# A graph network of four layers: six transfers a block moved to GpSimd's queue, a refinement in five VectorE operations, and diffusion halves added by GpSimd

## The chip, the core and the metric

The kernel runs on one core of one Trainium2 chip. A core has five engines with a queue each: TensorE (PE in the profile; its weight loads are PEld), VectorE (DVE), ScalarE (ACT), GpSimd (POOL) and SyncE (SP). Each queue is worked through in order, and semaphores make an instruction wait for another queue. Transfers between SBUF and HBM are issued from a queue (SP, ACT or POOL) and carried out by 16 DMA engines that all queues share. The metric is the device time of one execution in microseconds (us); lower is better.

## The reference

Input are 4096 nodes with 256 features and a 4096 x 4096 adjacency of zeros and ones. Four layers follow each other, each as `x = layernorm(x + layer(x, adj))`: an attention over neighbours with 8 heads (layer 0), a product with the adjacency (layer 1), the layer that matters here (layer 2), and a product with the adjacency divided by the degrees (layer 3). Layer 2 makes two steps:

```python
R = S + eye(N); R = R / R.sum(-1, keepdims=True)      # S is the adjacency
Xf = X; Xa = X; Z = 0
for n in range(2):
    A = top_p_attention(Xa, W1, W2, W3)
    Xf = R @ Xf
    Xa = A @ Xa
    Z = Z + Xf @ U1[n].T + Xa @ U2[n].T
h = layernorm(X + Z) * ln_g + ln_b
```

`top_p_attention` takes the softmax of all 4096 logits of a row, keeps the largest probabilities until their sum reaches 0.9, sets the others to zero and divides by the sum of what is kept. `R @ Xf` is called the diffusion below.

## The kernel before

The nodes are cut into 32 blocks of 128 rows. Layer 2 runs its two steps one after the other; in each, a loop over b goes through the blocks (`for b in range(NB - 1)`, under `tc.manual_schedule`, which keeps the instructions of PE, ACT, DVE and POOL in the order in which the program writes them). An iteration is a software pipeline with eight slots s = 0 to 7. In it

- the scores of block b+2 are made: four products (L933) of four matmuls on TensorE, two in slot 0 and two in slot 1, into PSUM tiles `ps_logit` of which there are two, and after each an exponential on ScalarE (L937) that writes 1024 columns of the row's weights `e` and sums them. The third product needs the tile that the first exponential has read, the fourth the second's;
- the threshold of block b+2 is guessed on ScalarE (`guessed`): a first cut c1 from the sum, two passes over `e` in two halves each (L1030, outputs `ja`), which give the count and the sum S1 above c1, and a chain of operations on one column (most through the helper `fma`, L946), which gives a better cut `c`. In step 2 a tail follows (L1052 to L1059), which makes the slopes `gw` and `sq` for one more refinement;
- the cut of block b+1 is settled on VectorE (`nucleus`). In step 2 it first takes the sum S2 of all weights above `c` in one pass of 4096 columns (L953), then refines the cut in seven operations on one column (L1077 to L1083) to `hi`. Then both steps gather the largest weights below `hi` (L1092, L1096, L1104, L1106), find by how many the sum 0.9 is reached (`bef` is the sum before them, L1112 and L1113, and so on to L1143), and zero what falls away (L1147);
- block b's weights are transposed on TensorE (L1286), copied by ScalarE (L1288, `aT`) and multiplied with X (L1295) into `ps_a`, of which there is one;
- the diffusion of block b+2 is made (L179) from pieces of the adjacency that SP's queue loads, into `ps_r`;
- the diffusion of block b+1 is finished (`diffused`): XD holds its operand split into a high and a low part, so that `ps_r` has two halves of 256 columns. ScalarE scales the low half (L1329), VectorE scales the high half and adds the low (L1331), and GpSimd adds the sum to `xb`, which `base` has loaded (L1317, L1332). In step 2 `keep` stores it (L1338);
- in step 2, block b-1 is closed (`closing`): ScalarE scales `ps_a` into `h` (L1434), GpSimd adds the loaded `xb` (`bases`, L1323; the add is L1438) and normalises twice with VectorE's statistics (L85, L86) and its own operations (L88, L89, L96, L1441, L1442); the result is stored (L1446). Block b-2 then makes its part of layer 3's operands (`turned`, `weighted`, `ahead3`; stores in L1457 and L1458).

So step 2 has six transfers a block beside those on SP's queue, and they are all issued from ScalarE's queue: L1338 in slot 4, L1457, L1458, L1317 and L1323 in slot 6, L1446 in slot 7. The tail of the guess runs where the loop finishes the generator at the head of slot 0, ahead of the scores:

```python
pa = ps1.tile([P, 512], F32, name="ps_a")
whole(guessing)
guessing = guessed(step, b + 2) if ahead else iter(())
if s < 2 and ahead:
    next(score)
    next(score)
```

Outside the block loops a scheduler orders the instructions.

Of the kernel before, what the change touches and what calls it, by code (L numbers as in the profile page):

```python
# [9 lines left out]
F32 = mybir.dt.float32  # L10
# [7 lines left out]
ALU = mybir.AluOpType  # L18
# [5 lines left out]
P = 128  # L24
# [31 lines left out]
class Net:  # L56
# [686 lines left out]
    def layer2(self):  # L743
# [3 lines left out]
        with ExitStack() as ctx:  # L747
# [40 lines left out]

            consts = [math.log(math.sqrt(2 * math.pi) / N), *QUANTILE, -FEW, 0.5 * N, 14.0, 0.75, 0.5, 400.0, CENTRAL[1]]
            cs = pool.tile([P, len(consts)], F32, name="cs")  # L790
# [178 lines left out]
            def guessed(step, b):  # L969
# [75 lines left out]

                c, gw, sq, lows = (small(n, bufs=2) for n in ("c3", "gw", "sq", "lows"))
                ic = small("ic")
                fma(c, low, -1.0, c2, AF.Relu)
                fma(c, c, 1.0, low)
                nc.scalar.mul(lows, c, 0.3)  # L1050
                yield c, lows, far, thr, S1, gw, sq
                nc.scalar.activation(ic, c, AF.Ln)  # L1052
# [8 lines left out]
            def nucleus(step, b, c, low, far, thr, S1=None, gw=None, sq=None):  # L1061

# [9 lines left out]
                if step == 0:  # L1072
                    nc.vector.tensor_scalar(hi, c, low, far, op0=ALU.max, op1=ALU.mult)
                else:
                    d = small("d")
                    S2 = evaluate("S2", e, c)
                    nc.vector.scalar_tensor_tensor(d, S1, S2, gw, op0=ALU.subtract, op1=ALU.mult)  # L1077
# [235 lines left out]
            def base(step, b):  # L1313


                xb = work.tile([P, 2, D], F32, name="xb", bufs=2)
                nc.scalar.dma_start(xb[:, 0], xd[b, :, 0, :] if step else pd[b])  # L1317
                return xb

            def bases(b):  # L1320

                xb = work.tile([P, 2, D], F32, name="xb", bufs=2)
                nc.scalar.dma_start(xb, xd[at(b)].rearrange("o p s d -> (o p) s d"))  # L1323
                return xb

            def diffused(b, pr, xb):

                dif = work.tile([P, D], F32, name="dif", bufs=1)
                nc.scalar.mul(dif, pr[:, D:], rdeg[:, at(b)])  # L1329
                yield  # L1330
                nc.vector.scalar_tensor_tensor(dif, pr[:, :D], rdeg[:, at(b)], dif, op0=ALU.mult, op1=ALU.add)  # L1331
                nc.gpsimd.tensor_add(xb[:, 0], xb[:, 0], dif)  # L1332

            def keep(step, b, xb):

                if step == 1:
                    yield
                    nc.scalar.dma_start(xd[b, :, 0, :], xb[:, 0])  # L1338
                    return
                part = work.tile([P, 2, D], F32, name="part", bufs=1).bitcast(F32R)  # L1340
                nc.scalar.copy(part[:, 0], xb[:, 0])
                yield
                nc.vector.tensor_sub(part[:, 1], xb[:, 0], part[:, 0].bitcast(F32))
                yield
                nc.scalar.dma_start(xfd[b], part.bitcast(F32))
# [83 lines left out]

            def closing(b, pa, r, xb, hand=None):  # L1430

# [17 lines left out]
            def ahead3(b, h, pz, last=False):  # L1449

                part = XD[:, b] if last else work.tile([P, 2, D], F32, name="part", bufs=1).bitcast(F32R)
                nc.scalar.copy(part[:, 0], pz[:, D:])
                nc.scalar.copy(h[:, 0], pz[:, :D])
                nc.vector.tensor_sub(part[:, 1], pz[:, D:], part[:, 0].bitcast(F32))
                yield
                if not last:
                    nc.scalar.dma_start(xtd[at(b)].rearrange("o p s d -> (o p) s d"), part.bitcast(F32))  # L1457
                nc.scalar.dma_start(xo[at(b), :, 1].rearrange("o p d -> (o p) d"), h[:, 0])  # L1458

# [11 lines left out]
            for step in range(2):  # L1471
# [25 lines left out]
                pr = whole(diffusion(step, 0))  # L1497
                whole(diffused(0, pr, xb))
                whole(keep(step, 0, xb))
# [5 lines left out]
                with tc.manual_schedule(engines={ET.PE, ET.Activation, ET.DVE, ET.Pool}):  # L1505
                    for b in range(NB - 1):
# [6 lines left out]
                        for s in range(8):  # L1513
                            if s == 0:
                                if b:
                                    if step == 0:
                                        store(b - 1, pa, rs.pop(b - 1))
                                    else:
                                        close = closing(b - 1, pa, rs.pop(b - 1), xc)
                                        next(close)  # L1520
                                difs = diffused(b + 1, pr, xb)
# [20 lines left out]
                            if s == 3 and step == 1 and b - 2 in done:  # L1542
                                put = ahead3(b - 2, done.pop(b - 2), pz)
                                next(put)
# [10 lines left out]
                            if s == 6:  # L1555
                                if ahead:
                                    xb = base(step, b + 2)
                                if step == 1:
                                    xc = bases(b)
                            if s >= 2 and ahead:  # L1560
# [169 lines left out]
```

## Time and profile before

| | us |
|---|---|
| median of 3 runs (4158.45 to 4166.36) | 4163.09 |
| the profiled execution | 4162.25 |
| its span, first to last instruction | 4160.5 |
| busy: PE, DVE, ACT, POOL | 3926.9, 3051.4, 2748.5, 958.6 |
| step 1's block loop, by the profile | about 1832 to 2720 |
| step 2's block loop, by the profile | about 2847 to 3861 |

A page of the profile gives busy time for each engine, groups of instructions by source line (L1295 is line 1295 of the kernel before), what ended an engine's idle time, and a timeline. "e<-e,edge" names an instruction by the tiles it writes and reads; ACTq or POOLq is the queue's own work, such as issuing a transfer. A wait for several semaphores is put down to the one that came last. Lines in step 2 that matter: L953 takes 4.49 us on VectorE each time, L1030 2.0 us on ScalarE, L937 1.02, L1438 3.97 on GpSimd with a shortest of 0.72.

### The profile page before, as it was taken

The page shows a single profiled execution, that of the slowest core. Times are in us where ns is not written, and L with a number is a line of the kernel's source. Part 1 is how long each engine was busy: PE and PEld are TensorE (multiplying, and loading weights), DVE is VectorE, ACT ScalarE, POOL GpSimd, SP SyncE. Part 2 cuts the span into 40 slices and gives each one's busy share as a digit, 9 for nine tenths or more (in the row PEclk, how much of TensorE's full clock was granted, in tenths as well). Part 3 has the DMA queues.
Part 4 walks back from the last instruction along what each step waited for, and adds up shares of the span by engine and source line. Part 5 has one row for each costly group of instructions (what it writes and reads, how often), then busy time and mean ns, then how long its engine had stood idle before and what let it go on. Part 6 is the DMA issues. An engine that isn't in the chain of part 4 may idle for free. (4 is left out here: it accounts for less than half of the span.)

```text
span 4160.5 us, 68601 instructions
## 1 busy us (share of the span) xinstructions
PE 3926.9 (94%) x25081; PEld 3380.1 (81%) x25081; DVE 3051.4 (73%) x6882; ACT 2748.5 (66%) x5103; POOL 958.6 (23%) x954
## 2 busy tenths in 40 slices
PE   7999989999997999799999999899999999998799
PEld 6999989999997787478888888656777777777587
DVE  7643239999998444658888888756999999999354
ACT  5543339999996322468888888545887878876232
POOL 0111110110333122200110110013444444444111
PEclk9999999999998999999999999999999999999899
DMA  4765554224320796333333333444333333334341
GB/s 124 226 206 179 177 200 158 80 82 164 91 71 18 282 377 232 91 120 101 94 96 102 95 94 104 147 130 122 103 96 102 102 108 102 97 102 150 133 136 46
DMA packets 303608, 545.13 MB, mean 131 GB/s; under 512 B 38294, under 2 KB 134038, under 8 KB 299158
## 3 DMA queue, kind: packets, MB, share of 16 engines
q1 hardware_dynamic: 200068, 367.08, 27.7%
q10 hardware_dynamic: 87506, 125.11, 8.8%
q0 software_dynamic: 15680, 48.38, 3.7%
q8 instruction: 203, 3.33, 0.3%
q14 instruction: 151, 1.24, 0.1%
HBM read 374.51 MB, written 165.94 MB: 130 GB/s over the span
## 5 line engine op out<-in xcount | busy, mean ns | idle before, releaser
L1295 PE MATMUL ps_a<-X,aT 128*128 128x256 f32 x4096 | 977.7, 381 | 17.4 <-ACT h L1434 15.3
L1295 PEld LDWEIGHTS ps_a<-X,aT 128*128 128x128 f32 x4096 | 772.6, 190 | 153.7 <-ACT h L1434 27.3
L300 PE MATMUL acc<-gm,gt 128*128 128x198 bf16 x8192 | 705.7, 249 | 26.1 <-issue 14.9
L300 PEld LDWEIGHTS <-gt 128*128 128x128 fp8e4 x8192 | 701.9, 97 | 29.9 <-issue 15.0
L292 ACT ACTIVATE sg<-lpb,nlc 128x1024 fp8e4<-128x1024 f32 x640 | 671.3, 1135 | 59.4 <-DVE gt L294 34.4
L179 PE MATMUL ps_r<-XD,adj_piece 128*128 128x512 f32 x2048 | 576.5, 416 | 8.1 <-DMA adj_piece<-adjs 5.0
L517 PE MATMUL pz<-src,ar 128*128 128x264 f32 x4096 | 511.4, 288 | 10.7 <-DVE ar L507 8.2
L517 PEld LDWEIGHTS pz<-src,ar 128*128 128x128 f32 x4096 | 508.4, 190 | 13.5 <-DVE ar L507 11.9
L1030 ACT ACTIVATE ja<-e,nc 128x2048 uint8<-128x2048 f32 x240 | 481.2, 2005 | 52.5 <-DMA xtd<-part 34.1
L1288 ACT COPY aT<-ps_tp 128x512 f32<-128x512 f32 x512 | 298.0, 582 | 246.6 <-PE ps_tp L1286 233.2
L179 PEld LDWEIGHTS ps_r<-XD,adj_piece 128*128 128x128 f32 x2048 | 364.5, 190 | 86.7 <-issue 14.3
L510 ACT ACTIVATE nb<-a 128x512 uint8<-128x512 f32 x256 | 156.6, 630 | 293.7 <-DMA a<-in_adjt_dram 287.1
L1096 DVE MAX8 cand<-v 128x8 f32<-128x256 f32 x1024 | 347.3, 414 | 4.4
L1147 DVE SCALAR_TENSOR_TENSOR e<-e,edge 128x512 f32<-128x512 f32 x512 | 344.9, 747 | 2.2
L203 ACT ACTIVATE adj_piece<-na 128x1024 fp32r<-128x1024 fp8e4 x128 | 135.3, 1059 | 317.9 <-PE ps_adj L731 132.7
L1286 PE MATMUL ps_tp<-ident,e 128*128 128x128 f32 x2048 | 309.8, 274 | 6.6 <-ACTq L1159 3.2
L933 PE MATMUL ps_logit<-kT,q 128*128 128x512 f32 x1024 | 276.7, 411 | 33.5 <-ACT e L937 27.3
L1092 DVE SCALAR_TENSOR_TENSOR v<-e,hi 128x2048 f32<-128x2048 f32 x128 | 305.9, 2390 | 2.3
L1286 PEld LDWEIGHTS ps_tp<-ident,e 128*128 128x128 f32 x2048 | 257.6, 142 | 60.6 <-issue 4.1
L285 DVE TENSOR_SCALAR sg<-lpb,nlc 128x1024 fp8e4<-128x1024 f32 x384 | 283.4, 775 | 2.0
L937 ACT ACTIVATE e<-ps_logit 128x1024 f32<-128x1024 f32 x256 | 259.5, 1023 | 19.0 <-PE ps_logit L933 17.1
L507 DVE CAST ar<-a 128x1024 fp32r<-128x1024 f32 x128 | 88.7, 693 | 230.7 <-PE pz L517 230.7
(341 smaller groups left out, 5445.9 us busy)
## 6 DMA issues: line engine op xcount, KB each, us to landing
adj_piece<-adjs SPq DMA_DIRECT2D x512, 256.0 KB
a<-in_adjt_dram SPq DMA_DIRECT2D x256, 256.0 KB
adjs<-adj_piece SPq DMA_DIRECT2D x96, 512.0 KB
na<-nad SPq DMA_DIRECT2D x64, 512.0 KB
na<-nad ACTq DMA_DIRECT2D x32, 1024.0 KB
nad<-nb POOLq DMA_DIRECT2D x128, 128.0 KB, 3.3
lpb<-lpd POOLq DMA_DIRECT2D x32, 512.0 KB, 4.3
gmd<-gb ACTq DMA_DIRECT2D x64, 198.0 KB
```

Of the source, the lines that this page charges most:

```text
L179: nc.tensor.matmul(ps, a[:, k, :], rhs(jc).rearrange("p s d -> p (s d)"), start=(jc == 0), stop=(jc == self.NB - 1))
L285: nc.vector.tensor_scalar(sg[:, k, :], lpb, nlc[:, jc, h:h + 1], 2.0 ** -5, op0=ALU.is_ge, op1=ALU.mult, saturate=False)
L292: nc.scalar.activation(sg[:, k, :], lpb, AF.Sign, scale=-1.0, bias=nlc[:, jc, h:h + 1], saturate=False)
L300: nc.tensor.matmul(acc[:, q, :6 * C1], gt[:, k, q * P:(q + 1) * P], gm[:, jc, hh, :], start=(jc == 0 and q % 2 == 0), stop=(jc == NB - 1 a ...
L517: nc.tensor.matmul(pz[q][:, t, :W], ar[:, q, k, :], src[:, jc, t, s], start=(jc == 0 and s == 0), stop=(jc == NB - 1 and s == 1))
L1030: nc.scalar.activation(ja, e[:, s * HALF:(s + 1) * HALF], f, bias=nc1, accum_out=fs[:, i + s:i + s + 1])
L1092: nc.vector.scalar_tensor_tensor(v, ec, hi, ec, op0=ALU.is_lt, op1=ALU.mult, accum_out=sb[:, s:s + 1])
L1096: nc.vector.max(cand[:, 8 * j:8 * j + 8], v[:, k * 256:(k + 1) * 256])
L1147: nc.vector.scalar_tensor_tensor(ec, ec, edge[:, j:j + 1], ec, op0=ALU.is_ge, op1=ALU.mult)
L1286: nc.tensor.transpose(pt[:, k * P:(k + 1) * P], e[:, jc * P:(jc + 1) * P], self.ident)
L1288: nc.scalar.copy(aT, pt)
L1295: nc.tensor.matmul(pa[:, :D], aT[:, k * P:(k + 1) * P], X[:, jc, :], start=(jc == 0), stop=(jc == NB - 1))
```

## The change

In step 2 the six transfers of a block are issued from GpSimd's queue. The refinement is written as `hi = max(c + (S2 - thr) * sq / (S2 * gw - pm), low) * far` with gw of the opposite sign and a new column pm = S1 * gw - 400 made by ScalarE: five VectorE operations instead of seven. The two operations of `bef` become one, in both steps. In step 2 ScalarE scales both halves of the diffusion in one operation of 512 columns, and GpSimd adds the halves to `xb` one after the other; VectorE no longer takes part. The tail of the guess is moved behind the first product and exponential of slot 0. `xT` has one buffer instead of two, and `dif` is twice as wide. What is left out below is one more constant (-400) and the new argument `step` or `queue` where these functions are called.

```diff
                 nc.scalar.mul(lows, c, 0.3)
-                yield c, lows, far, thr, S1, gw, sq
+                yield c, lows, far, thr, pm, gw, sq
                 nc.scalar.activation(ic, c, AF.Ln)
                 nc.scalar.activation(ic, ic, AF.Exp, scale=-1.0)
-                fma(gw, S1, 1.0, nthr)
+                fma(gw, S1, -1.0, thr)
                 nc.scalar.mul(gw, gw, ic)
                 nc.scalar.activation(sq, gw, AF.Square)
                 nc.scalar.mul(gw, gw, ic)
+                fma(pm, S1, gw, cs[:, 13:14])
                 fma(sq, sq, 1.0, cs[:, 11:12])
                 nc.scalar.mul(sq, sq, ri)
...
                     S2 = evaluate("S2", e, c)
-                    nc.vector.scalar_tensor_tensor(d, S1, S2, gw, op0=ALU.subtract, op1=ALU.mult)
-                    nc.vector.tensor_scalar_add(d, d, 400.0)
+                    nc.vector.tensor_scalar(d, S2, gw, pm, op0=ALU.mult, op1=ALU.subtract)
                     nc.vector.reciprocal(d, d)
-                    nc.vector.tensor_mul(d, sq, d)
-                    nc.vector.scalar_tensor_tensor(hi, S2, thr, d, op0=ALU.subtract, op1=ALU.mult)
-                    nc.vector.tensor_scalar(hi, hi, c, low, op0=ALU.add, op1=ALU.max)
-                    nc.vector.tensor_mul(hi, hi, far)
+                    nc.vector.tensor_scalar(hi, S2, thr, sq, op0=ALU.subtract, op1=ALU.mult)
+                    nc.vector.scalar_tensor_tensor(hi, hi, d, c, op0=ALU.mult, op1=ALU.add)
+                    nc.vector.tensor_scalar(hi, hi, low, far, op0=ALU.max, op1=ALU.mult)
...
-                nc.vector.scalar_tensor_tensor(bef[:, 0:1], sb[:, 0:1], -1.0, Z, op0=ALU.mult, op1=ALU.add)
-                nc.vector.tensor_sub(bef[:, 0:1], bef[:, 0:1], sb[:, 1:2])
+                nc.vector.tensor_scalar(bef[:, 0:1], Z, sb[:, 0:1], sb[:, 1:2], op0=ALU.subtract, op1=ALU.subtract)
...
-                nc.scalar.dma_start(xb[:, 0], xd[b, :, 0, :] if step else pd[b])
+                if step:
+                    nc.gpsimd.dma_start(xb[:, 0], xd[b, :, 0, :])
+                else:
+                    nc.scalar.dma_start(xb[:, 0], pd[b])
                 return xb
 
-            def bases(b):
+            def bases(b, queue=nc.scalar):
...
-                nc.scalar.dma_start(xb, xd[at(b)].rearrange("o p s d -> (o p) s d"))
+                queue.dma_start(xb, xd[at(b)].rearrange("o p s d -> (o p) s d"))
...
-            def diffused(b, pr, xb):
-
-                dif = work.tile([P, D], F32, name="dif", bufs=1)
-                nc.scalar.mul(dif, pr[:, D:], rdeg[:, at(b)])
+            def diffused(step, b, pr, xb):
+
+                dif = work.tile([P, 2, D], F32, name="dif", bufs=1)
+                if step == 1:
+                    nc.scalar.mul(dif.rearrange("p s d -> p (s d)"), pr, rdeg[:, at(b)])
+                    yield
+                    for s in (1, 0):
+                        nc.gpsimd.tensor_add(xb[:, 0], xb[:, 0], dif[:, s])
+                    return
+                nc.scalar.mul(dif[:, 1], pr[:, D:], rdeg[:, at(b)])
                 yield
-                nc.vector.scalar_tensor_tensor(dif, pr[:, :D], rdeg[:, at(b)], dif, op0=ALU.mult, op1=ALU.add)
-                nc.gpsimd.tensor_add(xb[:, 0], xb[:, 0], dif)
+                nc.vector.scalar_tensor_tensor(dif[:, 0], pr[:, :D], rdeg[:, at(b)], dif[:, 1], op0=ALU.mult, op1=ALU.add)
+                nc.gpsimd.tensor_add(xb[:, 0], xb[:, 0], dif[:, 0])
...
                 if step == 1:
                     yield
-                    nc.scalar.dma_start(xd[b, :, 0, :], xb[:, 0])
+                    nc.gpsimd.dma_start(xd[b, :, 0, :], xb[:, 0])
                     return
...
-                xT = work.tile([P, 2, P], F32, name="xT")
+                xT = work.tile([P, 2, P], F32, name="xT", bufs=1)
...
-                nc.scalar.dma_start(xo[at(b), :, 0].rearrange("o p d -> (o p) d"), hb)
+                queue.dma_start(xo[at(b), :, 0].rearrange("o p d -> (o p) d"), hb)
...
-                    nc.scalar.dma_start(xtd[at(b)].rearrange("o p s d -> (o p) s d"), part.bitcast(F32))
-                nc.scalar.dma_start(xo[at(b), :, 1].rearrange("o p d -> (o p) d"), h[:, 0])
+                    queue.dma_start(xtd[at(b)].rearrange("o p s d -> (o p) s d"), part.bitcast(F32))
+                queue.dma_start(xo[at(b), :, 1].rearrange("o p d -> (o p) d"), h[:, 0])
...
                                 pa = ps1.tile([P, 512], F32, name="ps_a")
-                                whole(guessing)
-                                guessing = guessed(step, b + 2) if ahead else iter(())
+                                if not ahead:
+                                    whole(guessing)
+                                    guessing = iter(())
                             if s < 2 and ahead:
                                 next(score)
+                                if s == 0:
+                                    whole(guessing)
+                                    guessing = guessed(step, b + 2)
                                 next(score)
```

More of the change, by code (lines that the diff above doesn't have):

```diff
@@ L787, in layer2 @@
             kT = pool.tile([P, N], F32R, name="kT")
-            consts = [math.log(math.sqrt(2 * math.pi) / N), *QUANTILE, -FEW, 0.5 * N, 14.0, 0.75, 0.5, 400.0, CENTRAL[1]]
+            consts = [math.log(math.sqrt(2 * math.pi) / N), *QUANTILE, -FEW, 0.5 * N, 14.0, 0.75, 0.5, 400.0, CENTRAL[1], -400.0]
             cs = pool.tile([P, len(consts)], F32, name="cs")
@@ L1043, in guessed @@
                     return
-                c, gw, sq, lows = (small(n, bufs=2) for n in ("c3", "gw", "sq", "lows"))
+                c, gw, sq, pm, lows = (small(n, bufs=2) for n in ("c3", "gw", "sq", "pm", "lows"))
                 ic = small("ic")
@@ L1057, in guessed, with nucleus @@
                 nc.scalar.mul(gw, gw, ic)
+                fma(pm, S1, gw, cs[:, 13:14])
                 fma(sq, sq, 1.0, cs[:, 11:12])
                 nc.scalar.mul(sq, sq, ri)
-            def nucleus(step, b, c, low, far, thr, S1=None, gw=None, sq=None):
+            def nucleus(step, b, c, low, far, thr, pm=None, gw=None, sq=None):
                 e = es[b % 3][:, :N]
@@ L1428, in store, with closing @@
                 nc.scalar.dma_start(xad[at(b)].rearrange("o p d -> (o p) d"), h[:, 0])
-            def closing(b, pa, r, xb, hand=None):
+            def closing(b, pa, r, xb, hand=None, queue=nc.scalar):
                 h = work.tile([P, 1, D], F32, name="h", bufs=3)
@@ L1445, in closing, with ahead3 @@
                 yield
-                nc.scalar.dma_start(xo[at(b), :, 0].rearrange("o p d -> (o p) d"), hb)
+                queue.dma_start(xo[at(b), :, 0].rearrange("o p d -> (o p) d"), hb)
                 return h
-            def ahead3(b, h, pz, last=False):
+            def ahead3(b, h, pz, last=False, queue=nc.scalar):
                 part = XD[:, b] if last else work.tile([P, 2, D], F32, name="part", bufs=1).bitcast(F32R)
@@ L1497, in layer2 @@
                 pr = whole(diffusion(step, 0))
-                whole(diffused(0, pr, xb))
+                whole(diffused(step, 0, pr, xb))
                 whole(keep(step, 0, xb))
@@ L1518, in layer2 @@
                                     else:
-                                        close = closing(b - 1, pa, rs.pop(b - 1), xc)
+                                        close = closing(b - 1, pa, rs.pop(b - 1), xc, queue=nc.gpsimd)
                                         next(close)
-                                difs = diffused(b + 1, pr, xb)
+                                difs = diffused(step, b + 1, pr, xb)
                                 next(difs)
@@ L1542, in layer2 @@
                             if s == 3 and step == 1 and b - 2 in done:
-                                put = ahead3(b - 2, done.pop(b - 2), pz)
+                                put = ahead3(b - 2, done.pop(b - 2), pz, queue=nc.gpsimd)
                                 next(put)
@@ L1558, in layer2 @@
                                 if step == 1:
-                                    xc = bases(b)
+                                    xc = bases(b, nc.gpsimd)
                             if s >= 2 and ahead:
```

## The prediction

> **What bounds the kernel now.** First I read the stretches of 104 us, to find the second step of layer 2 and to see which engine is full there. Columns: stretch, its length, then busy time of PE, PEld, DVE, ACT and POOL, each with its count, the granted clock, the DMA share and GB/s. The first row is from step 1's block loop, the second from step 2's.
>
> ```profile
> 2288.00:2392.00 104.00, 104.00 (x527) 88.60 (x526) 87.00 (x249) 88.90 (x195) 11.82 (x8) 1.00 0.31 95
> 3328.00:3432.00 104.00, 99.99 (x486) 81.33 (x486) 97.30 (x260) 82.87 (x195) 43.47 (x34) 1.00 0.36 107
> ```
>
> In step 1 TensorE never rests, so nothing the change does there can count. In step 2 TensorE has gaps and VectorE is nearly full. The starts of L1077, one a block, give the period: 32.36 us, constant within 0.3 us over 26 blocks in a row (starts from 2954.79 to 3796.49). So I ask what closes this period. The list of waits over 2915 to 3815 us (28 blocks; columns: total us, times, longest):
>
> ```profile
> ACT aT L1288 <- PE ps_tp L1286: 85.3, 84, 1.6
> ...
> ACT ja L1030 <- DMA xtd<-part: 34.1, 25, 1.5
> ...
> PE ps_logit L933 <- ACT e L937: 23.2, 28, 0.9
> DVE v L953 <- ACT c L946: 16.1, 26, 0.9
> ...
> PE ps_a L1295 <- ACT h L1434: 13.0, 26, 0.8
> ```
>
> Both TensorE waits and the one VectorE wait (0.6 us a block) end on ScalarE, and ScalarE itself loses 1.36 us a block under the name of a DMA. The timeline of ScalarE in one block shows what that is (start, length, instruction):
>
> ```profile
> 3234.31 0.34 ACTq L1457 DMA_DIRECT2D xtd<-part  x1
> 3234.69 0.44 ACTq L1458 DMA_DIRECT2D xo<-h  x1
> 3235.25 0.40 ACTq L1317 DMA_DIRECT2D xb<-xd  x1
> 3235.69 0.46 ACTq L1323 DMA_DIRECT2D xb<-xd  x1
> 3236.19 2.01 ACT L1030 ACTIVATE ja<-e,nc 128x2048 uint8<-128x2048 f32 x1 [1.35 <-DMA xtd<-part]
> ...
> 3242.23 0.48 ACT L1434 ACTIVATE h<-ps_a,inv 128x256 f32<-128x256 f32 x1
> 3242.59 0.47 ACT L1329 ACTIVATE dif<-ps_r,rdeg 128x256 f32<-128x256 f32 x1
> 3242.95 0.21 ACT L1052 ACTIVATE ic<-c 128x1 f32<-128x1 f32 x1
> ...
> 3244.89 1.00 ACT L937 ACTIVATE e<-ps_logit 128x1024 f32<-128x1024 f32 x1
> ```
>
> Not a landing but four issues, one after the other on ScalarE's queue, block it: its next work starts when the last issue ends. Everything down to the first exponential is then 1.35 us late. The two TensorE gaps of the same block:
>
> ```profile
> 3242.76 1.99 PE L1295 MATMUL ps_a<-X,aT 128*128 128x256 f32 x8 [0.49 <-ACT h L1434]
> ...
> 3246.04 2.20 PE L933 MATMUL ps_logit<-kT,q 128*128 128x512 f32 x8 [0.85 <-ACT e L937]
> ```
>
> The loop that sets 32.36 us is therefore: TensorE products, ScalarE's chain (guess, four issues, h, dif, the tail of the guess from L1052 to L1059, exponential), TensorE again. VectorE follows with 0.6 us to spare. Last, VectorE and GpSimd after the 4096-wide pass L953, which ends at 3246.13:
>
> ```profile
> 3246.25 0.50 DVE L1077 SCALAR_TENSOR_TENSOR d<-S,S,gw 128x1 f32<-128x1 f32 x1
> ...
> 3248.08 0.48 DVE L1331 SCALAR_TENSOR_TENSOR dif<-ps_r,rdeg,dif 128x256 f32<-128x256 f32 x1
> 3248.48 0.42 DVE L85 BATCH_NORM_STATS2 ln_stats<-h 128x6 f32<-128x256 f32 x1
> ```
>
> ```profile
> 3242.79 3.95 POOL L1438 TENSOR_TENSOR h<-h,xb 128x256 f32<-128x256 f32 x1 [11.22 <-ACT h L1434]
> ```
>
> The add L1438 needs 0.72 us (its shortest) but lasts until 3246.74, 0.6 us after L953; L1077, which should take 0.15 us like its neighbours, ends at 3246.75 with it.
>
> **What the Trainium skill says.** "SBUF — State Buffer", section "Who interferes with whom": a VectorE instruction with two SBUF inputs contends with a GpSimd instruction that reads SBUF, and whoever starts first holds the shared pair for its whole instruction. The last two fences agree in both directions: L953 holds up L1438 for 3.2 us, L1438 holds up L1077 for 0.35 us. The same page, "SBUF: two separate sides", warns that descriptors of a GpSimd-issued DMA cannot be written while VectorE runs in a two-port mode. The trace shows no harm from two-input instructions: in layer 0, 22 of the 32 loads of L234 fell under the two-input L287 alone and took 0.56 us, as all do (0.567).
>
> **The change, part by part**, in the time frame of this block.
>
> Six transfers leave ScalarE's queue. The four in a row give back 1.35 us; the other two (L1338, L1446) lie under a running aT copy and give back nothing. Without the 1.35 us, ScalarE reaches the aT copy of 3241.76 at 3240.40, but its transposes on TensorE start at 3239.80 and last 0.60: from there on ScalarE is tied to TensorE, at 3240.44. So the whole 1.35 us is just usable.
>
> From there ScalarE's new order is aT, h, dif, first exponential, tail of the guess, second exponential. Steps from start to start: aT 0.47, h 0.36, dif now 512 wide 0.56 (a 512-wide copy takes 0.20 more than a 256-wide one: 0.579 against 0.379), exponential 1.00. The tail took 1.94 (3242.95 to 3244.89); the new pm, dependent on gw, and the sq that follows cost 0.43 more (two steps of 0.33 and 0.30 in place of one of 0.20): 2.37. h ends at 3241.39, before TensorE is ready for it, so the ps_a gap goes (0.57 counted from start to start). The first exponential ends at 3242.83 and the third product no longer waits. But the fourth product needs the second exponential: 3240.44 + 0.47 + 0.36 + 0.56 + 1.00 + 2.37 + 1.00 = 3246.20, and 0.15 for the hand-over as now (3245.89 to 3246.04): 3246.35. Before, the fourth product started 1.02 after the third, at 3247.06. **Gain 0.7 us a block.** TensorE would have come to it at 3245.30 unhindered, so about 1.05 us of wait stays, moved from the third product to the fourth. The new period is 32.36 - 0.71 = 31.65.
>
> VectorE must fit in that. Now its period without the wait for c is 32.36 - 0.58 = 31.78. L1331 goes (0.40 start to start); two bef operations of 0.18 + 0.19 become one with two scalars, like L1082, 0.31 (gain 0.06). The refinement takes 1.83 from L1077 to L1331 now. New: the first operation reads one tensor and isn't held by L1438, 0.31; reciprocal 0.10, since the next does not depend on it; hi 0.31, and then hi*d+c, which again has two tensors. It is ready 0.84 us after L953, when GpSimd has just begun the first of its two added adds (L1438 ends at 0.61, the add at about 1.4), so it is held for some 0.5 us: 0.75 in all; the last 0.31. Sum 1.78, nearly what it was. VectorE's new period is 31.78 - 0.40 - 0.06 - 0.05 = 31.27, under 31.65. Bounds: with no hold 0.5 less (30.8), held by both adds 0.7 more (32.0).
>
> GpSimd gets two 0.73 us adds for one, and six issues. Rows here: 0.63 (L740, 128 KB), 0.73 (L1415, 256 KB), so 4.0 us a block. They sit after the second normalisation (ends 3230.2) with GpSimd idle until 3242.79, 11.22 us of cover. The xb load also waits for the xd store's landing (2.7 to 3.5 us in GpSimd's rows): store issued 3230.3, landed 3233.9; then 0.7 + 0.7 + landing 3.5 puts the last load at 3238.8. L1438 can't run before 3246.1 anyway. Without that cover each late us would stall VectorE's L85 by as much. What is queued behind these waits on GpSimd is only the next xo store and L1438. xT with one buffer costs nothing: one use a block. SP's queue keeps its order; only which landings it names differs.
>
> Steps 1 and the rest: bef in step 1 is hidden under TensorE (104.00 of 104.00).
>
> **Sum**, against the profiled execution (4162.25 us, span 4160.5; median of the runs 4163.09, 0.8 above it). 26 full blocks by 0.71: 18.5. Two early blocks (31.33 and 31.65, VectorE dense, few issues) by about 0.45: 0.9. The loop's entry, where a product waits 3.14 us for L1331 (2848.77), by its 0.48 and its hand-over: 0.8. The last block and the tail on VectorE alone, two by 0.5: 1.0. Together 21 us: span 4139, execution 4141, on the median's scale 4142.
>
> **Rivals.** (1) VectorE becomes the bound because both adds hold hi*d+c: 32.0 a block, gain 0.35, 10 us in all: 4153. For it: L1077's half microsecond. Against it: VectorE asks before the second add is ready. (2) The second exponential comes earlier than I count, for example because ScalarE is not tied to the transposes of 3239.80; then VectorE's 31.27, or at best 30.8, binds: 1.1 to 1.5 by 27, gain 30 to 42 us: 4127. For it: my 1.05 us wait rests on nine small steps. Against: ScalarE's 85.3 us of waits on transposes. (3) The regained ScalarE time is waited away again at the transposes, and the longer dif and pm eat the rest: gain 0.2 a block or less: about 4158. For it: 3.0 us a block of such waits already; against: none of them lies between the last aT and the exponentials. (4) Slower: GpSimd's descriptors are held while VectorE runs L1147 and L953 (3235.65 to 3246.13). If the xb pair is not out before 3235.65, it is issued at 3246.2, lands 4.2 later at 3250.4, the h add ends at 3251.1, and L85 waits 3.0 us: 31.27 + 3.0 = 34.3 a block, +1.9 by 29: 4218. It decides once a landing is later than 3246. Against it: the layer 0 loads above; for it: the loads wait for a store's landing first.
>
> **Numbers.** My forecast (13 to 27 us gained) 0.52; (1) 0.17; (2) 0.16; (3) 0.08; (4) 0.07. 0.2% is 8.3 us, about what a measurement of this kernel can tell from no change. Faster by more: the forecast, (2) and most of (1), 0.83; within it 0.10; slower 0.07. Range: the forecast, (1) and most of (2): 4122 to 4156.
>
> **What would show it.** Right: no DMA-named wait on ScalarE before ja; no PE wait on h; a PE wait on e of about a microsecond, now ahead of the fourth product; starts of the first refinement operation 31.6 to 31.7 apart; that operation near 0.3 and hi*d+c near 0.6. Wrong: VectorE waiting for h at L85, GpSimd waiting for xb, a period at 32.0 with VectorE gapless, or no PE wait left.

## The result, and the profile after

| | before | after |
|---|---|---|
| median of 17 runs each, side by side, us | 4162.57 | 4152.37 |
| the profiled execution, us | 4162.25 | 4152.52 |
| its span, us | 4160.5 | 4150.8 |
| period of step 2's block loop (median, refinement to refinement), us | 32.36 | 31.68 |

The ratio of the medians is 0.9977 (95% interval 0.9969 to 0.9984): faster by 10 us, half of the 21 us that I forecast. 4152 lies in the range given, but the forecast of a gain of 13 to 27 us failed. The period came out as I had it, 31.68 us for 31.65, so the missing half is not in the loop.

The stretch of step 2 that the prediction showed, in the kernel after (same columns):

```profile
3328.00:3432.00 104.00, 100.22 (x492) 82.16 (x490) 96.35 (x233) 88.69 (x218) 59.57 (x56) 1.00 0.32 99
```

TensorE has a little less idle time, VectorE a little less work, and GpSimd 16 us more: 22 more instructions, adds and transfers. The list of waits of the kernel after, over the same 2915 to 3815 us:

```profile
PE ps_logit L933 <- ACT e L937: 27.9, 28, 1.0
...
DVE v L953 <- ACT c L946: 26.3, 28, 3.4
...
POOL xb L1324 <- DMA xd<-xb: 3.0, 2, 2.4
...
PE ps_a L1293 <- ACT h L1441: 1.1, 1, 1.1
```

ScalarE's 34.1 us of waits ahead of `ja` have gone from the list, and TensorE's wait for `h` is down from 26 times to one. One TensorE wait of about 1 us a block is left (27.9 / 28), and its place shows in one block of the timeline, TensorE, ScalarE and VectorE in order of time:

```profile
3300.05 0.48 ACT L1441 ACTIVATE h<-ps_a,inv 128x256 f32<-128x256 f32 x1
3300.42 0.69 ACT L1331 ACTIVATE dif<-ps_r,rdeg 128x512 f32<-128x512 f32 x1
...
3300.99 1.03 ACT L937 ACTIVATE e<-ps_logit 128x1024 f32<-128x1024 f32 x1
...
3301.98 0.22 ACT L1052 ACTIVATE ic<-c 128x1 f32<-128x1 f32 x1
...
3303.32 1.18 PE L933 MATMUL ps_logit<-kT,q 128*128 128x512 f32 x4
...
3304.04 0.27 DVE L1078 TENSOR_SCALAR d<-S,gw,pm 128x1 f32<-128x1 f32 x1
...
3304.35 1.00 ACT L937 ACTIVATE e<-ps_logit 128x1024 f32<-128x1024 f32 x1
...
3304.79 0.42 DVE L1081 SCALAR_TENSOR_TENSOR hi<-hi,d,c 128x1 f32<-128x1 f32 x1
...
3305.50 1.19 PE L933 MATMUL ps_logit<-kT,q 128*128 128x512 f32 x4 [1.00 <-ACT e L937]
```

The third product (3303.32) starts without a wait, the fourth stands 1.00 us for the second exponential, which the tail of the guess (3301.98 to 3304.35) holds back.

Where the time went between the two traces, cut at events that both have:

| stretch | gain, us | forecast, us |
|---|---|---|
| up to the third pass L953 of step 2 (the loop's entry) | -1.0 | +0.8 |
| from there over 28 blocks | +18.3 | +19.4 |
| last block, and the tail up to layer 3's operand | -0.1 | +1.0 |
| layer 3, to the last store's issue | -0.7 | 0 |
| from that issue to the end of the program | -6.75 | 0 |
| sum | 9.7 | 21 |

Each row compares one execution with one. The loop's row is firm: in the seven kernels below that keep the old loop the 28 blocks take 904.7 to 905.0 us, for 904.7 here, and 886.4 after. The entry and the last block are not. Eight kernels that do the same work up to step 2's first refinement (the changed one and the seven built on it) reach it between 2786.1 and 2792.1 us, and the last block takes 34.18 us after but 31.68 in a version that differs only in where the tail stands.

The row before the sum is the surprise. The end of the timeline, first of the kernel before, then of the one after; the last line of each is the last instruction that this view lists:

```profile
core 0 of [0], span 4160.5 us
...
4157.82 0.34 ACTq L1661 DMA_DIRECT2D out_dram<-y  x1
```

```profile
core 0 of [0], span 4150.8 us
...
4141.37 0.34 ACTq L1672 DMA_DIRECT2D out_dram<-y  x1
```

The same last store is followed by 2.70 us before and by 9.45 us after. No engine works in it, and the chain that ended last stops ahead of it. The records of the trace that the views leave out, because they count as no work, name it: at the end of the program each engine runs a DRAIN on its queue. SyncE's is done at 4143.65; GpSimd's takes 2.264 us in the kernel before and 9.69 us in the one after (from 4140.28). In the kernel before it ended at 4158.99, 0.7 us ahead of SyncE's (4159.69), so of the 7.4 us that it grew by, 6.75 lengthen the program. The time is lost at the end of the program, on the queue that received the transfers.

### The profile page after: what moved, and what is told of

It is laid out like the page before. It is cut to its first block, busy times and chain, and to the rows that moved or that the text cites. A ratio compares the mean times of both kernels' runs of the same rounds, so it can differ in the third digit from the quotient of the medians.

```text
span 4150.8 us, 68616 instructions
## 1 busy us (share of the span) xinstructions
PE 3914.5 (94%) x25081; PEld 3378.5 (81%) x25081; DVE 3027.3 (73%) x6723; ACT 2768.8 (67%) x5135; POOL 1075.7 (26%) x1169
```

## The experiments

Two questions: which part of the change gains in the loop, and what makes the drain long. "The last drain" below is GpSimd's long DRAIN at the end (two of 0.11 and 0.04 us follow it), from the profiled execution of each run.

### Which part gains

**Transfers alone**: the kernel before, with its six transfers issued from GpSimd and nothing else.

```diff
-                nc.scalar.dma_start(xb, xd[at(b)].rearrange("o p s d -> (o p) s d"))
+                queue.dma_start(xb, xd[at(b)].rearrange("o p s d -> (o p) s d"))     # queue = nc.gpsimd; likewise the other five
```

> The kernel before with the six transfers of a step 2 block on GpSimd's queue and nothing else. Theory (the loop is closed by ScalarE, and what was lost of the gain sits at the end of the program, where GpSimd's last DRAIN took 9.69 us instead of 2.26): ScalarE comes 1.35 us earlier, the exponentials too, and VectorE with its old work of 31.78 us binds: period 31.7 to 31.9 us, and the DRAIN at the end again near 9.7. In all 8 to 10 us faster than before. Rival (the edits of VectorE's work carry the gain): period stays above 32.2, and the time is no better than before.

Measured: 4154.28 (before 4162.77), ratio 0.998 [0.9973, 0.9986], period 31.72, last drain 9.692. All but some 2 us of the gain, and all of the drain. Its list of waits shows another closing link:

```profile
PE ps_tp L1286 <- DVE e L1147: 12.7, 27, 0.5
...
PE ps_logit L933 <- ACT e L937: 8.4, 28, 0.3
```

TensorE now waits mainly for VectorE, and VectorE's wait for `c` (16.1 us before) is gone from the list: with its old work VectorE is the bound, at 31.72.

**All but the transfers**: the changed kernel, with the six on ScalarE's queue as before.

```diff
-                    nc.gpsimd.dma_start(xb[:, 0], xd[b, :, 0, :])
+                    nc.scalar.dma_start(xb[:, 0], xd[b, :, 0, :])     # likewise the other five
```

> The changed kernel with the six transfers back on ScalarE's queue, the rest kept. Theory: ScalarE is 1.35 us late again and has 0.63 us more to do ahead of the second exponential, so the fourth product waits longer: period 32.9 to 33.1 us, last DRAIN back at 2.3 us, 12 to 20 us slower than before. Rival (VectorE's lighter work carries the gain): period below 32, and about 15 us faster than before, since the DRAIN is gone.

Measured: 4175.27, ratio 1.0037 [1.0023, 1.005], period 32.99, last drain 2.264. Slower than before, and by its waits it is ScalarE that is late:

```profile
PE ps_logit L933 <- ACT e L937: 43.2, 28, 1.6
ACT ja L1030 <- DMA xtd<-part: 35.4, 26, 1.5
```

With the four issues still in a row, the wider `dif` and the longer tail lie on the path in full: +0.63 us a block.

**Tail in its old place**: the changed kernel, with the tail ahead of slot 0's scores.

```diff
-                                if not ahead:
-                                    whole(guessing)
-                                    guessing = iter(())
+                                whole(guessing)
+                                guessing = guessed(step, b + 2) if ahead else iter(())
                             if s < 2 and ahead:
                                 next(score)
-                                if s == 0:
-                                    whole(guessing)
-                                    guessing = guessed(step, b + 2)
                                 next(score)
```

> The changed kernel with the tail of the guess ahead of the first product's exponential again, as before. Theory: the second exponential ends at the same moment in either order, so only the wait moves back from the fourth product to the third: period 31.7 us and the time of the changed kernel within 0.1%. Rival (the move of the tail is part of the gain): period 32.3 or more, all of the gain lost.

Measured: 4152.52, ratio 0.9977 [0.9969, 0.9985], period 31.69: no difference from the change. The wait is back at the third product (0.93 us in the block at 3301.53); in either place the tail stands ahead of the second exponential, and the fourth product comes as late.

**Tail behind both exponentials**: the changed kernel, one step further.

```diff
                             if s < 2 and ahead:
                                 next(score)
+                                next(score)
                                 if s == 0:
                                     whole(guessing)
                                     guessing = guessed(step, b + 2)
-                                next(score)
```

> The changed kernel with the tail of the guess moved one step further, behind the second product's exponential. Theory (the period is closed by ScalarE's work ahead of the second exponential): both exponentials of slot 0 then end before TensorE asks for their tiles, the wait of about 1.0 us a block goes, and TensorE's own 30.7 us bind, or VectorE with pm coming 1 us later: period 30.7 to 31.0, 18 to 27 us faster than the changed kernel, last DRAIN unchanged at 9.7. Rival (something else closes the loop at 31.68, such as VectorE): period stays 31.6 or grows, because pm and sq come later.

Measured: 4125.31 (before 4163.28), ratio 0.9909 [0.9893, 0.9926], period 30.73. TensorE's waits for `e` are gone from the list, and 104 us of its loop are nearly all TensorE:

```profile
3500.00:3604.00 104.00, 103.64 (x512) 85.56 (x511) 99.30 (x238) 91.15 (x225) 64.93 (x58) 1.00 0.32 101
```

So the 1 us a block that the change left at the fourth product was the tail's, and moving it off gives 0.95 us a block.

**The same with VectorE's old work**: that kernel with the refinement in seven operations, `bef` in two and the diffusion finished by VectorE, as before. ScalarE's `pm` and its wider `dif` go back with them.

```diff
-                    nc.vector.tensor_scalar(d, S2, gw, pm, op0=ALU.mult, op1=ALU.subtract)
+                    nc.vector.scalar_tensor_tensor(d, S1, S2, gw, op0=ALU.subtract, op1=ALU.mult)
+                    nc.vector.tensor_scalar_add(d, d, 400.0)
...
-                    for s in (1, 0):
-                        nc.gpsimd.tensor_add(xb[:, 0], xb[:, 0], dif[:, s])
+                nc.vector.scalar_tensor_tensor(dif, pr[:, :D], rdeg[:, at(b)], dif, op0=ALU.mult, op1=ALU.add)
```

> The kernel before with the six transfers on GpSimd's queue and the tail of the guess behind both exponentials, VectorE's refinement, bef and diffusion as before (e8 without the VectorE edits). Theory (VectorE's edits are worth nothing while ScalarE holds the loop at 31.7, and about 1 us a block once it does not): VectorE's old work of 31.7 to 31.8 us a block binds, so period 31.7 to 31.9, about 25 us slower than e8. Rival (VectorE's edits never matter): period 30.7 to 31.0 as in e8.

Measured: 4155.12 (before 4164.68), ratio 0.9976 [0.9968, 0.9984], period 31.73, the same as the transfers alone. VectorE is the bound again, without a wait for `c`:

```profile
PE ps_tp L1286 <- DVE e L1147: 30.8, 28, 1.2
```

VectorE's part of the change is thus worth almost nothing in this change (transfers alone 31.72, the whole 31.68), because ScalarE's tail then holds the loop, and 1.0 us a block where the tail doesn't.

**SyncE's queue**: the changed kernel, with the six issued by SyncE.

```diff
-                    nc.gpsimd.dma_start(xb[:, 0], xd[b, :, 0, :])
+                    nc.sync.dma_start(xb[:, 0], xd[b, :, 0, :])     # likewise the other five
```

> The changed kernel with the six transfers on SyncE's queue instead of GpSimd's. Theory: ScalarE is as free as in the changed kernel, so the period stays 31.7 us, and the last DRAIN of GpSimd falls back to 2.3 us because nothing new is issued there: 7 us faster than the changed kernel, 16 to 17 faster than before. Rival (the DRAIN's length has nothing to do with where the transfers are issued): DRAIN stays at 9.7 and the time equals the changed kernel's. A loss would come from adjacency pieces that stand behind a store's wait on SyncE's queue: then TensorE waits at the diffusion.

Measured: 4158.12 (before 4162.77), ratio 0.9988 [0.9981, 0.9994], period 31.95 (31.68 in many blocks), last drain 2.262. The drain is short again, but SyncE also feeds TensorE with the adjacency, and there it comes late:

```profile
PE ps_r L179 <- DMA adj_piece<-adjs: 7.2, 11, 2.7
```

In the change these waits were 2.7 us, 4 times. The last block takes 39.83 us, for 34.18 in the change and 31.68 with the tail in its old place.

### What makes the drain long

The kernels below issue spare transfers from GpSimd that nobody reads; they add work and leave nothing out. The first three stand on the kernel before: 180 of 128 KB in layer 3, 186 of them in step 1's block loop, and 180 of 64 bytes in layer 3.

```diff
+                for k in range(6 if b < NB - 2 else 0):
+                    nc.gpsimd.dma_start(spare[b, k], bias)      # the tiny ones: spare[b, k, :1, :16], bias[:1, :16]
```

> The kernel before with 180 added transfers of 128 KB that nobody reads, issued from GpSimd in layer 3, six a block, none in its last two blocks. If the length of the last DRAIN follows the number of transfers issued from GpSimd: 9 to 10 us. If it follows something else of the changed kernel (control flow, reuse of semaphores in step 2): it stays at 2.3.

> The kernel before with 186 added transfers of 128 KB that nobody reads, issued from GpSimd in step 1 of layer 2, six a block, over 1400 us before the end. If the DRAIN pays for every transfer of the program: 9 to 10 us. If only for recent ones, or for those after the last control flow: 2.3.

> The kernel before with 180 added transfers of one row of 64 bytes that nobody reads, issued from GpSimd in layer 3 in the same places. If the DRAIN pays for each transfer: as long as with 128 KB each. If it pays for the rows or bytes moved: near 2.3.

Then half of the late ones, 183 early ones, and six of 128 KB in layer 3 on top of the version with the tail behind both:

> The kernel before with 90 added transfers of 128 KB that nobody reads, issued from GpSimd in layer 3, three a block: 334 in all. If the DRAIN grows in proportion to the transfers issued late: half of the 7.2 us that 180 added, so about 5.9 us. If it is a sawtooth over the number of all transfers: any length up to 10 us, other than 5.9.

> The kernel before with 183 added transfers of 128 KB that nobody reads, issued from GpSimd in step 1 of layer 2: 427 in all, as in the changed kernel, but over 1400 us before the end. If the number of all transfers decides: DRAIN 9.7 us. If how late they are issued decides: 1.8 to 2.3 us.

> The kernel of e8 (tail behind both exponentials) with six added transfers of 128 KB that nobody reads, issued from GpSimd in layer 3, two in each of its blocks 2 to 4: 433 transfers from GpSimd in the program instead of 427. The last DRAIN was 2.26 us at 244 transfers, 9.45 at 424, 9.69 at 427 (the same to 2 ns in three kernels), and 1.77 at 430. If it is a sawtooth over the number of transfers, growing by 0.08 us each and falling back between 427 and 430: DRAIN 1.8 to 2.2 and some 7 us faster than e8, less what six issues disturb in layer 3. If it pays for recent transfers only: 9.7 or more, and no gain.

Two counts in these expectations were off: the early loop covers one more block than I had reckoned, so 192 and 189 were added, not 186 and 183 (436 and 433 in all, not 430 and 427). The second was chosen to reach the kernels' own 427 and missed it, on the other side of a fall that the next table shows.

With what I had learnt from these, a pair to be timed, the kernel before with 71 and with 91 early spare ones:

```diff
+                for k in range(3 if b < 23 else 2 if b == 23 else 0):     # 71; the other: 3 if b < 30 else 1 if b == 30 else 0, 91
+                    nc.gpsimd.dma_start(spare[b, k], affine)
```

> The kernel before with 71 spare transfers of 128 KB, which nobody reads, issued by GpSimd in step 1's block loop: 315 transfers of GpSimd in all. By the saw-tooth that the earlier runs draw (0.082 us more for each transfer, a fall about every 106), the last drain is between 8.5 and 9.4 us in the profiled execution. If the executions without a profile carry the same drain, the median is 6 to 7 us above the run with 335 transfers beside it, and about 6.5 above the kernel before; if the drain only shows under the profiler, it is the same as that one's within 2 us.

> The same with 91 spare transfers, 335 in all, 20 more than its neighbour: last drain about 2.2 us in the profiled execution, as the run with 334 had it (2.097), and the median within 2 us of the kernel before. If what costs is the transfers themselves, it is slower than its neighbour with 71.

All of them by the number of transfers that GpSimd issues in the program:

| kernel | GpSimd's transfers | last drain, us | profiled execution, us | median, us (runs) |
|---|---|---|---|---|
| before | 244 | 2.264 | 4162.25 | 4162.57 (17) |
| 71 spare early | 315 | 8.058 | 4165.02 | 4168.94 (13) |
| 90 spare late | 334 | 2.097 | 4179.62 | |
| 91 spare early | 335 | 2.178 | 4158.67 | 4163.34 (13) |
| 180 spare late | 424 | 9.447 | 4203.61 | |
| 180 tiny ones late | 424 | 7.082 | 4190.52 | |
| transfers alone; after; tail in old place; tail behind both; that with old VectorE work | 427 | 9.69 | | 4154.28; 4152.37; 4152.52; 4125.31; 4155.12 |
| 189 spare early | 433 | 1.525 | 4164.16 | |
| tail behind both, six spare late | 433 | 1.523 | 4116.3 | 4125.43 (4) |
| 192 spare early | 436 | 1.77 | 4159.14 | |

The drain grows by 0.082 us for each transfer (2.097 to 2.178, 1.525 to 1.77, 9.447 to 9.69) and falls back by some 8 us between 315 and 334 and between 427 and 433: a saw-tooth in the number of transfers issued over the whole program. From 244 to 315 and from 335 to 424 the same 0.082 us a transfer comes out. The number is not all: with 64-byte transfers the drain is 7.08 us at 424, for 9.45 with 128 KB ones, which neither of the two expectations for that run had. How the size enters is open. When they were issued makes no difference (433 early and 433 late agree to 2 ns); the idea that the last transfers were still under way at the end is excluded by that. Late ones also cost layer 3 time of their own, which is why three of the executions are so long.

The pair asks whether executions without a profile pay too. The kernel with 20 more transfers is 5.6 us faster by the medians, 5.1 by the means (95%: 2.9 to 7.3). In the profiled executions the drains differ by 5.9 us, and the time from the last store's issue to the end by 5.1 (7.80 and 2.69), since the start of a drain lies beside other work. So in this pair they pay. (The drain at 315 was 8.06, a little under the 8.5 to 9.4 that I expected; against the kernel before, the medians are 4.4 us up and 1.2 down.) One run does not fit: the six spare transfers on the version with the late tail took 8 us off the profiled execution, 6.3 of them after the last store's issue, but its other three executions took 4124.65 to 4127.31, as without them. Why is open, and so is what the queue does in the drain.

**The loop's gain without GpSimd's transfers**: the changed kernel, its six transfers back on ScalarE's queue, the stores L1464 and L1465 issued a slot earlier, so that two issues stand in a row and not four. And the same with the tail behind both exponentials.

```diff
-                    nc.gpsimd.dma_start(xb[:, 0], xd[b, :, 0, :])
+                    nc.scalar.dma_start(xb[:, 0], xd[b, :, 0, :])     # likewise the other five
...
-                            if s == 6 and put:
+                            if s == 5 and put:
```

> The changed kernel, but its six transfers a block go back to ScalarE's queue, and the two stores of block b-2 are issued in slot 5 instead of slot 6, so that no more than two issues stand in a row, each pair behind an aT copy that has to wait for TensorE anyway. My theory (the gain in the loop comes from ending the row of four issues, not from GpSimd's queue as such; the missing 7 us are GpSimd's last drain, which grows with what GpSimd has issued): period 31.6 to 31.8 as in the changed kernel, last drain back at 2.3 us (244 transfers issued by GpSimd, as before), execution about 4145, 7 us under the changed kernel. Rival (ScalarE loses the time of its issues wherever they stand): period 32.4 or more, about 4162.

> The same with the tail of the guess behind the second exponential as well. My theory: period 30.7 to 31.0, last drain 2.3 us, execution 4117 to 4121, that is 5 to 7 us under the version with the transfers on GpSimd's queue (4125.3). Rival (with the tail gone, ScalarE is tight elsewhere and the issues cost their 2.6 us): period 31.5 or more, 4140 or more.

Measured: 4146.4 (before 4164.56), ratio 0.9958 [0.9944, 0.9971], period 32.02, last drain 2.264; and 4116.49, ratio 0.9883 [0.9868, 0.9899], period 30.68 (30.75 and 30.62 in turn), last drain 2.264. The first one's period is 0.2 longer than I expected, between my theory and the rival: the pair of loads still holds `ja` for some 0.4 us.

```profile
3297.36 0.45 ACTq L1324 DMA_DIRECT2D xb<-xd  x1
3297.85 2.00 ACT L1030 ACTIVATE ja<-e,nc 128x2048 uint8<-128x2048 f32 x1 [0.37 <-issue]
```

Its five executions spread from 4144.24 to 4154.47, with the profiled one (4152.73) near the top. In that one the 28 blocks take 894.6 us, 8 more than in the change, which the shorter end of the program (2.7 us for 9.45) does not quite make up. So that it is faster than the change at all is not sure. The second is: 4116.49, 48 us under the kernel before beside it and some 9 under the same version with the transfers on GpSimd, of which the ends of the program make up 6.75 in the profiled executions. It is the best of all that were run. The row for its loop shows TensorE full:

```profile
3500.00:3604.00 104.00, 103.72 (x511) 85.50 (x510) 98.94 (x242) 90.63 (x223) 58.37 (x44) 1.00 0.33 102
```

## Why the prediction was half right

**The bound and the loop: right, in size too.** Six transfers gone from ScalarE: the wait before `ja` went, and with the transfers alone the loop already fell to 31.72. The chain of steps on ScalarE held in each: from the start of the transposes (3298.93) to `aT` 0.64, to `h` 0.48, to `dif` 0.37, to the first exponential 0.57, to the tail 0.99, through the tail 2.37, to the fourth product 1.15; counted were 0.64, 0.47, 0.36, 0.56, 1.00, 2.37 and 1.15. The wait left at the fourth product is 1.0 for 1.05, the period 31.68 for 31.65. Over the 28 blocks 18.3 us came of 19.4; a few blocks take 32.0 to 32.3.

**VectorE: the direction right, the size not.** `hi*d+c` takes 0.42 us in a usual block (0.22 at its shortest, 0.72 at most), so GpSimd's add holds it for about 0.2 us, not 0.5: the Trainium skill's rule ("SBUF — State Buffer", "Who interferes with whom") shows here in a one-column operation, but for less than I allowed. In the block above the add had already run 0.31 us of its 0.72 (from 3304.48), and the two end within 0.02 us of each other. For L1077, too, I had the free time too short: an operation of its form with two tensors took 0.22 us in the kernel before (L1081), not 0.15, so L1438 held it for about 0.28 us. VectorE waits 0.85 us a block for `c` (22.9 us in 27 times over 2950 to 3780), so its own period is about 30.8, my lower bound. Rival (1) fell. VectorE is the bound only with its old work, at 31.72 and 31.73 for the 31.78 that I had worked out for it.

**GpSimd's queue: right about the loop, wrong at its entry (below).** The six issues take 0.54 to 0.65 each, 3.4 us a block where I had 4.0:

```profile
3319.34 0.65 POOL L1345 DMA_DIRECT2D xd<-xb  x1
...
3320.95 0.55 POOL L1464 DMA_DIRECT2D xtd<-part  x1 [0.32 <-ACT nthr L1009]
3321.50 0.54 POOL L1465 DMA_DIRECT2D xo<-h  x1
3322.03 0.55 POOL L1316 DMA_DIRECT2D xb<-xd  x1
3322.56 0.55 POOL L1324 DMA_DIRECT2D xb<-xd  x1
3323.11 0.55 POOL L1453 DMA_DIRECT2D xo<-h  x1
```

In the loop they lie in GpSimd's idle time and have landed (4.8 us after the issue, median) before L1445 wants `xb`; GpSimd waited for a landing twice in the whole stretch (3.0 us). Rivals (3) and (4) fell; no issue in the loop took longer than 0.66 us.

**Rival (2) fell for the change.** ScalarE was tied to the transposes as counted. The version with the tail behind both exponentials comes to 4125 for this rival's 4127, but by another way: the second exponential is earlier because the tail is behind it, and TensorE is the bound, not VectorE.

**The step that failed is the sum**, in two of its terms and in one that was not there.

- Not there, and the largest: the end of the program. The sum put it at nothing; 6.75 us came back between the last store's issue and the end, because GpSimd's last drain grew by 7.4 us with its 183 more transfers. I costed these at issue and at landing, and no line of the page told that they are paid a third time. The profile before had the drain of 2.264 us for 244 transfers, which said nothing of its course. Shown: the drain depends on the number of transfers (table above). That executions without a profile pay for it is shown by the timed pair alone, with one run against it; the change's own medians, 10.2 us apart, agree with its profiled executions, 9.7 apart.
- The loop's entry, forecast +0.8, gave -1.0: 2.7 us lost ahead of step 2's first refinement, 3.5 gained up to the second, 1.9 lost up to the third. The first two lie where executions differ by themselves (the second stretch took 43.2 us here and 40.7 in the seven other kernels with the old loop). The third comes from the change. The prediction said that behind the waits of GpSimd's queue stand only the next store and L1438. At the entry there is more: the first block's load waits 4.67 us there for a store's landing, and behind it stands GpSimd's last add of the stage before, L1428. ScalarE issues the store of that add (at 2847.51, for 2846.21 before) ahead of `dif`, so `dif` starts 0.73 us later, and the product of the diffusion later instead of earlier. Of the kernel after:

```profile
2845.59 0.59 POOL L1316 DMA_DIRECT2D xb<-xd  x1 [4.67 <-DMA xd<-xb]
2846.20 1.27 POOL L1428 TENSOR_TENSOR xb<-xb,part 128x512 f32<-128x512 f32 x1
```

  The product, before and after:

```profile
2848.77 4.52 PE L179 MATMUL ps_r<-XD,adj_piece 128*128 128x512 f32 x12 [3.14 <-DVE dif L1331]
```

```profile
2849.20 4.94 PE L179 MATMUL ps_r<-XD,adj_piece 128*128 128x512 f32 x12 [5.29 <-ACT dif L1331]
```

  TensorE waits 5.3 to 6.4 us here in all six kernels with these transfers on GpSimd's queue, and at most 3.1 in the eleven with them on ScalarE's.

- The last block and the tail, forecast +1.0, gave -0.1: the last block takes 34.18 us for 32.74, with TensorE waiting for pieces of the adjacency (0.6 and 1.4 us) and VectorE 3.4 us for `c`; what follows gained 1.3. Why those pieces come late was not tested; with 31.68 in the version with the tail in its old place, it need not be the change.

That 4152.37 lies in the range, and beside rival (1)'s 4153, is luck: the loop gained as forecast, and what took half of it back was in no rival.

And the forecast priced the change as one thing. That VectorE's part and the move of the tail bring next to nothing in this change (transfers alone 4154.28, tail in the old place 4152.52, the whole 4152.37) could be read from its own numbers: with its old work it gave VectorE 31.78, nearly the 31.65 at which ScalarE's longer chain then holds the loop, and the tail stayed ahead of the second exponential.

## What to carry to other kernels

A transfer moved to another queue can cost more than its issue. On a queue that is worked through in order, a load that waits for a store's landing holds up all that stands behind it (4.67 us at the loop's entry here): look at the entry as well as at the loop. On GpSimd it can also be paid for at the end of the program: compare the time from the last store's issue to the span's end before and after, since no busy time shows it. A row of issues on a compute engine's queue blocks that engine as its work does (four took 1.35 us a block here). In pairs, without another queue, they gave half of the loop's gain while the tail stood between the exponentials (32.02), and all of it once the tail stood behind both (30.7 on either queue). And where an exponential frees a tile that TensorE waits for, put what nobody waits for behind the last such exponential, not behind the first (0.95 us a block).

## What was not expected of the hardware

- GpSimd's drain at the end of the program: 1.5 to 9.7 us, 0.082 us more for each transfer that it has issued, with falls of some 8 us (between 315 and 334, and between 427 and 433), early or late transfers alike. Tiny transfers (64 bytes) gave 7.08 where as many of 128 KB gave 9.45. It starts beside the program's last work, so about the first 3 us of it are covered: drains of 1.5 to 2.3 us left 2.7 to 3.1 us from the last store's issue to the end, one of 9.69 left 9.45.
- Transfers on ScalarE's and SyncE's queues don't lengthen it: with the same six a block there, GpSimd's drain is 2.26 us.
